# A transformer block on images: the first layer norm without its mean, the projection put into the attention's weights

## Chip, cores and metric

The kernel runs on one core of a Trainium2 chip, in fp32. The metric is the device time in microseconds of one execution; the kernel before takes 4315.69 us (median of 3 runs, 4314.87 to 4317.05). The profiled execution has a span of 4311.6 us. The core's engines are named as in the profile: PE (TensorE, matmuls and transposes), DVE (VectorE), ACT (ScalarE), POOL (GpSimd), SP (SyncE, which here only issues DMAs).

## The reference

x has 16 images of 128 channels by 96 x 96 pixels. Per image:

```python
xn1 = layernorm(x over channels) * ln1_w + ln1_b
q, k, v = xn1 @ wq.T, xn1 @ wk.T, xn1 @ wv.T      # 8 heads of 16 channels
q, k = l2norm over all 9216 pixels
attn = softmax(q @ k.T * scale)                   # 16 x 16 per head: channels, not pixels
x = x + (attn @ v) @ wp.T
xn2 = layernorm(x over channels) * ln2_w + ln2_b
h1 = w_in @ xn2                                   # 1x1, 128 -> 512 channels
h2 = depthwise 3x3 of h1
x = x + w_out @ gelu(h2)                          # 1x1, 512 -> 128 channels
```

The attention mixes channels, so an image needs of q and k only the Gram matrix of its normed pixels: G = sum over pixels of z z^T, and the sum s of z, with z the normed pixel. Everything up to the mixing matrix then is arithmetic on 128 x 128 matrices, once per image.

## The kernel before, in words

*Layout.* x lies with channels in the partitions. A layer norm is over channels, so pixels are turned into the partitions, normed there, and turned back. Both norms are made by one function, `norm(i, second, ...)`; norm a (`second` false) is LN1, norm b is LN2. Norm a of an image runs while the feed-forward network of the image before is computed, norm b a few bands ahead of its own image's network.

*One batch of a norm* is 4 tiles of 128 pixels; an image has 18 batches, and all 16 images 288 per norm. Its steps, with the name of the kind and the line of the profile:
- `forth`, PE L552: four transposes into a PSUM tile pT (two buffers).
- `stats`, DVE L559: two instructions that each give count, mean and variance sums of two tiles.
- `variance` and `power`, POOL L566 and L570: ve = var + eps, rstd = ve ** -0.5, four numbers per partition.
- `shift`, DVE L574: nb = -mean * rstd, four numbers per partition.
- `scaled`, ACT L591: zT = Identity(pT * rstd + nb), one activation per tile with two per-partition operands, scale and bias. In the first image's norm a, and in the first five batches of its norm b, DVE makes half of the tiles (L583, subtract mean, multiply by rstd).
- norm a only: `gram`, PE L601: G and s accumulate in one PSUM bank from zT with a column of ones.
- `back` and `place`, PE L631 and ACT L637 (norm a, plain copy) or L635 (norm b, with bias b2): zT turned back, 384 pixels at a time, and written as z into the padded buffers xn.

*Attention* (once per image, L697 to L796) goes from G and s over several small products on PE, copies on DVE, a power on POOL and one Exp on ACT to the mixing matrix mwT = w1 * (wv^T y) and to the vector d = (wv^T y)^T b1. Its weights are prepared once, by `weights`: wqkT is the transposed wq and wk with w1 multiplied in, cqk are the biases that b1 gives.
*Mixing* (L510): PE multiplies mwT with z, and d and x are added by ACT (L519) and a DMA that accumulates, or by DVE (L516).

*The feed-forward network* works on bands of 12 rows, 128 in all, in four chunks of 128 hidden channels. PE makes the hidden channels (L821), ACT copies them to SBUF (L826, `kept`). A 3x3 depthwise convolution is nine taps: ACT makes a few as products (L837, one into h3, two or three into buffers pr that a DMA adds), DVE makes the rest (L841, one instruction of 1152 elements per tap). ACT applies gelu (L849). In 66 of the 128 bands the fourth chunk is made by PE instead (L892, nine accumulated products, gelu at L898). PE multiplies with w_out (L915) and DVE adds x (L922).

*The order.* Nothing of this is ordered by a queue at run time. `Plan` collects every piece of work with its engine, a cost in ns, the tokens that it reads and writes and a place; the place is a job number plus an offset per kind from the table `AT`. `order()` simulates the engines: whenever one is free it takes the ready piece with the smallest place, where a piece is ready when its inputs are there (with a `SLACK` of 300 ns between engines) and its buffer is free. The program is written in that order, and each engine then runs its own instructions in this order. So the offsets in `AT`, the costs given to `dve(...)`, `act(...)`, `pe(...)`, and the buffers (two for pT, four PSUM banks h, three zT, five pr) decide what stands behind what.

Of the kernel before, what the change touches and what calls it, by code (L numbers as in the profile page):

```python
# [9 lines left out]
F32 = mybir.dt.float32  # L10
# [21 lines left out]
AT = dict(  # L32
    weights=11.05, zeros=-2.3, load_a=-22.85, forth_a=-15, stats_a=-11, variance_a=-7.95, power_a=3.5,
    shift_a=-15.95, scaled_a=-2.85, gram=-4.15, back_a=-20.9, place_a=-21.85, attention=-18.15, mix=-8.5,
    residual=-15.95, mixed=-8.45, add_x=12.05, forth_b=-12.4, stats_b=-8.15, variance_b=-11.85,
    power_b=-15.9, shift_b=-27.4, scaled_b=2.2, back_b=-22.2, place_b=-0.25, halo=6.25, hidden=0.55,
    kept=-7.05, product=-12.5, products=4.05, add_last=-15.5, tap=1.25, add_first=23.45, gelu=-16.4,
    conv=-0.5, conv_gelu=-14.15, out=3.65, add=-2.4, store=-0.9,
)
# [166 lines left out]
def tile_restormer_block(  # L206
# [21 lines left out]


    nc = tc.nc  # L230
    B, C, H, W = x.shape
# [48 lines left out]
    nc.scalar.dma_start(out=dw, in_=w_dw.rearrange("(n p) o kh kw -> p n (o kh kw)", p=P))  # L280

    none = const.tile([P, 1], F32, name="none")
    wqkT = const.tile([P, 2 * P], F32, name="wqkT")
# [113 lines left out]
    def weights(p):  # L397
# [4 lines left out]
        def loads():  # L402
            a, b = (h3p.tile([P, BR * W], F32, tag="h3", name=f"weights_{k}") for k in range(2))
            v["win"] = a[:, :HID].rearrange("p (n c) -> p n c", c=P)
            v["wout"], v["wp"] = a[:, HID : 2 * HID], a[:, 2 * HID : 2 * HID + P]
            v["wqk"], v["wqkT"] = b[:, : 2 * P], b[:, 2 * P : 4 * P]
            v["wt"] = b[:, 4 * P : 8 * P].rearrange("p (t c) -> p t c", c=P)
            nc.scalar.dma_start(out=v["wqk"][:, :P], in_=wq)
            nc.scalar.dma_start(out=v["wqk"][:, P:], in_=wk)
            nc.scalar.dma_start(out=v["wp"], in_=wp)  # L410
            nc.scalar.dma_start(out=v["win"], in_=w_in.rearrange("(n p) c kh kw -> p n (c kh kw)", p=P))
            nc.scalar.dma_start(out=v["wout"], in_=w_out.rearrange("c j kh kw -> c (j kh kw)"))
# [15 lines left out]
        def keep_qkp(pt):  # L428
            nc.vector.tensor_copy(v["wqkT"], pt[:, : 2 * P])
            nc.vector.tensor_scalar(wqkT, pt[:, : 2 * P], w1, None, ALU.mult)  # L430
            nc.vector.tensor_copy(wpT, pt[:, 2 * P : 3 * P])

        def biases():
# [9 lines left out]
        def shifts():  # L443
# [9 lines left out]
        transposed(  # L453
            lambda: [v["wqk"][:, :P], v["wqk"][:, P:], v["wp"]], keep_qkp, ["qk"]
        )
        pe(440, at("weights", p), biases, [("w", "qk"), mine[1]], [("h", ("weights", "biases"))])
        dve(400, at("weights", p), lambda: nc.vector.tensor_copy(cqk, v["pc"]), [("h", ("weights", "biases"))], [("w", "qk")])
        transposed(
            lambda: [v["win"][:, n, :] for n in range(NCH)],
# [34 lines left out]
    def norm(i, second, place_of):  # L494
# [41 lines left out]
        def pixels(s, m):  # L536
# [43 lines left out]
            def also_scaled(q):  # L580
                for k in range(by_dve):
                    t = (q - qs[0]) * QT + k
                    nc.vector.tensor_scalar(  # L583
                        zT(q)[:, k, :P], d["pT", q][:, k, :], d["mv"][:, t, 1:2], d["rstd"][:, t : t + 1],
# [3 lines left out]
            def scaled(q):  # L588
                for k in range(by_dve, QT):
                    t = (q - qs[0]) * QT + k  # L590
                    nc.scalar.activation(  # L591
                        zT(q)[:, k, :P], d["pT", q][:, k, :], AF.Identity,
# [20 lines left out]
            op("POOL", T_POWER, at("power" + ab, s), power, [], [bt], T_POWER + 33 + SLACK)  # L613
            dve(80, at("shift" + ab, s), shift, [], [bt])
            for h, (q, tr) in enumerate(zip(qs, trs)):
                zt, sh = ("zT", (name, q)), s + STEP["scaled"] * h
                if by_dve:
                    dve(by_dve * 240, at("scaled" + ab, sh), lambda q=q: also_scaled(q), [tr, bt], [(*zt, 0)])
                act((QT - by_dve) * 343, at("scaled" + ab, sh), lambda q=q: scaled(q), [tr, bt], [(*zt, 1)])
                if not second:  # L620
# [48 lines left out]
    def attention(s, i):  # L669


        places_of = dict(srow="ma", kq="ma", em="ma", y="ma", gs="mb", e="mb", a="mb", mT="mb")
        columns = dict(ps_s=128, ps_u=256, ps_r=0, ps_n=128, ps_kq=256, ps_qk=384, ps_y=0, ps_m=128, ps_d=256)
# [105 lines left out]

        @step("PE", 220)  # L780
        def _():
            nc.tensor.matmul(ps([P, P], "ps_m"), lhsT=wv_sb, rhs=v["y"], start=True, stop=True)

        @step("DVE", 400)
        def _():
            nc.vector.tensor_scalar(sb([P, P], "mwT", keep), v["ps_m"], w1, None, ALU.mult)
            nc.vector.tensor_copy(sb([P, P], "mT"), v["ps_m"])

        @step("PE", 220)
        def _():  # L790
            nc.tensor.matmul(ps([P, 1], "ps_d"), lhsT=v["mT"], rhs=b1, start=True, stop=True)

        @step("DVE", 80)
        def _():
            nc.vector.tensor_copy(sb([P, 1], "d", keep), v["ps_d"])
# [204 lines left out]
```

## Time and profile before

| | PE | DVE | ACT | POOL |
|---|---|---|---|---|
| busy, us | 4216.3 | 4190.5 | 4149.9 | 2427.5 |
| share of the span | 98% | 97% | 96% | 56% |
| instructions | 17446 | 5086 | 7256 | 2309 |
| share of the chain that ended last | 46% | 13% | 32% | 2% |

Busy time is the time in which at least one instruction of the engine is under way. Instructions of one engine overlap at their ends, so an engine's busy time is more than the sum of the steps from one start to the next. The chain that ended last is followed back from the last instruction: at each step to what released it, or to the instruction before it on its engine. PE's granted clock is 0.996 of full speed on the mean. The DMA engines are at 0.90 of their time in the long middle of the run, mostly with the products that are added by DMA.

The groups of norm a, with the busy time of each, from the profile's groups:

| kind | engine, line | count | busy us | mean ns of one |
|---|---|---|---|---|
| forth | PE L552 | 1080 | 164.8 | 276 |
| stats | DVE L559 | 540 | 228.0 | 423 |
| variance | POOL L566 | 288 | 286.2 | 994 |
| power | POOL L570 | 288 | 497.0 | 1726 |
| shift | DVE L574 | 288 | 44.8 | 156 |
| scaled | ACT L591 | 1080 | 434.2 | 569 |
| gram | PE L601 | 2304 | 306.8 | 276 |
| place | ACT L637 | 384 | 227.1 | 591 |

(72 tiles of the first image are in groups of their own for forth and stats, and 36 more activations for scaled. A product in fp32 is two passes of PE, so gram has two per tile.)

### The profile page before, as it was taken

The numbers are of one execution on the slowest core, as the hardware profiler recorded it, in microseconds if no ns is written. First come the engines' busy times: TensorE is split into PE (matmuls) and PEld (weight loads), VectorE is DVE, ScalarE is ACT, GpSimd is POOL, SyncE is SP. The second block draws the span as 40 slices with busy tenths as digits, with TensorE's granted clock in tenths as the row PEclk, the third lists the DMA queues.
The fourth block names the chain that finished last, engine by engine and source line by source line (L and its number), as shares of the span: only waits on it lengthen the run. The fifth ranks groups of instructions, "written<-read, shape, count | busy, mean of one in ns | idle before, by whom it ended". The sixth has DMA issues, their size and how long they took to land.

```text
span 4311.6 us, 52468 instructions
## 1 busy us (share of the span) xinstructions
PE 4216.3 (98%) x17446; PEld 2686.8 (62%) x17446; DVE 4190.5 (97%) x5086; ACT 4149.9 (96%) x7256; POOL 2427.5 (56%) x2309
## 2 busy tenths in 40 slices
PE   8999999999999999999999999999999999999999
PEld 6666666666666666666666666666666666666555
DVE  6999999999999999999999999999999999999999
ACT  5999999999999999999999999999999999999996
POOL 3555556555565655656556555655655556556342
PEclk9999999999999999999999999999999999999999
DMA  2889898998989999889898998989989898888887
GB/s 85 174 182 197 184 188 183 187 193 183 190 179 191 192 185 190 188 187 194 183 189 179 194 192 182 191 175 194 194 180 194 176 200 184 185 185 175 178 182 165
DMA packets 194719, 789.89 MB, mean 183 GB/s; under 512 B 22544, under 2 KB 23952, under 8 KB 194448
## 3 DMA queue, kind: packets, MB, share of 16 engines
q0 software_dynamic: 154944, 634.72, 78.0%
q1 hardware_dynamic: 37152, 151.01, 9.6%
q8 instruction: 138, 2.26, 0.2%
q10 hardware_dynamic: 2352, 0.81, 0.1%
q14 instruction: 133, 1.09, 0.1%
HBM read 148.26 MB, written 75.50 MB: 52 GB/s over the span
## 4 chain that ended last, share of the span: by engine, by line
PE 46%; ACT 32%; DVE 13%; DMA 4%; issue 3%; POOL 2%; ACTq 0%; POOLq 0%; DVEq 0%
PE h L915 13%; PE h L892 12%; DVE h L841 10%; PE h L821 9%; ACT pr L837 8%; ACT zT L591 6%; ACT h L826 4%; ACT h L837 4%; ACT h L849 4%; DMA h<-pr 4%; PE g L601 3%; PE h L510 2%; ACT x L519 2%; PE pB_a L631 1%; ACT xn L635 1%
## 5 line engine op out<-in xcount | busy, mean ns | idle before, releaser
L841 DVE SCALAR_TENSOR_TENSOR h<-h,dw,h 128x1152 f32<-128x1152 f32 x2614 | 3593.6, 1407 | 2.8 <-ACT h L837 1.2
L837 ACT ACTIVATE pr<-h,dw 128x1152 f32<-128x1152 f32 x954 | 1291.4, 1369 | 3.8 <-DMA pr<-pr 3.7
L892 PE MATMUL h<-xn,comp 128*128 128x384 f32 x3564 | 1284.7, 487 | 3.5 <-DVE x L922 2.5
L915 PE MATMUL h<-h,woutT 128*128 128x384 f32 x3072 | 1143.9, 493 | 25.3 <-ACT h L826 17.0
L821 PE MATMUL h<-xn,winT 128*128 128x384 f32 (+1 forms) x2676 | 1047.3, 502 | 13.4 <-ACT h L826 7.5
L892 PEld LDWEIGHTS h<-xn,comp 128*128 128x128 f32 x3564 | 653.3, 189 | 430.7 <-issue 27.1
L915 PEld LDWEIGHTS h<-h,woutT 128*128 128x128 f32 x3072 | 562.0, 192 | 385.9 <-issue 28.5
L845 POOL DMA_DIRECT2D pr<-pr x509 | 480.5, 944 | 521.0 <-ACT pr L837 434.1
L826 ACT COPY h<-h 128x384 f32<-128x384 f32 (+1 forms) x1338 | 712.2, 588 | 39.0 <-PE h L821 26.2
L845 POOL DMA_DIRECT2D h<-pr x445 | 427.7, 963 | 562.7 <-DVE h L841 139.9
L821 PEld LDWEIGHTS h<-xn,winT 128*128 128x128 f32 x2676 | 485.9, 190 | 333.8 <-issue 28.4
L837 ACT ACTIVATE h<-h,dw 128x1152 f32<-128x1152 f32 x446 | 602.1, 1350 | 1.7
L849 ACT ACTIVATE h<-h 128x1152 f32<-128x1152 f32 x448 | 561.8, 1254 | 32.1 <-DMA h<-pr 28.4
L570 POOL TENSOR_TENSOR rstd_b<-ve_b,mhalf 128x4 f32<-128x4 f32 x288 | 513.8, 1784 | 11.8
L570 POOL TENSOR_TENSOR rstd_a<-ve_a,mhalf 128x4 f32<-128x4 f32 x288 | 497.0, 1726 | 13.5 <-POOL ve_a L566 0.2
L566 POOL TENSOR_SCALAR ve_b<-st_b 128x4 f32<-128x4 f32 x288 | 298.2, 1035 | 326.9 <-DVE st_b L559 321.3
L591 ACT ACTIVATE zT<-pT_b,nb_b,rstd_b 128x128 f32<-128x128 f32 x1132 | 454.2, 566 | 5.1 <-DVE nb_b L574 4.9
L566 POOL TENSOR_SCALAR ve_a<-st_a 128x4 f32<-128x4 f32 x288 | 286.2, 994 | 291.5 <-DVE st_a L559 287.5
L591 ACT ACTIVATE zT<-pT_a,nb_a,rstd_a 128x128 f32<-128x128 f32 x1080 | 434.2, 569 | 9.9 <-DVE nb_a L574 9.5
L601 PE MATMUL g<-zT 128*128 128x129 f32 x2304 | 306.8, 276 | 0.0
L510 PE MATMUL h<-xn,mwT 128*128 128x384 f32 x768 | 295.5, 490 | 4.1 <-ACT h L826 2.9
L601 PEld LDWEIGHTS g<-zT 128*128 128x128 f32 x2304 | 286.1, 192 | 15.3 <-issue 2.1
(145 smaller groups left out, 3761.0 us busy)
## 6 DMA issues: line engine op xcount, KB each, us to landing
pr<-pr POOLq DMA_DIRECT2D x509, 576.0 KB, 6.2
h<-pr POOLq DMA_DIRECT2D x445, 576.0 KB, 6.9
x<-in_x_dram SPq DMA_DIRECT2D x128, 576.0 KB, 6.0
out_dram<-x SPq DMA_DIRECT2D x127, 576.0 KB, 5.3
x<-in_x_dram POOLq DMA_DIRECT2D x122, 576.0 KB, 7.2
out_dram<-x SPq DMA_DIRECT2D x3, 192.0 KB, 1.9
weights<-in_L_conv_w_in_dram ACTq DMA_DIRECT2D x1, 256.0 KB, 10.8
weights<-in_L_conv_w_out_dram ACTq DMA_DIRECT2D x1, 256.0 KB, 11.7
```

Source lines behind the costliest of these rows:

```text
L566: nc.gpsimd.tensor_scalar(ve, d["mv"][:, :, 2], 1.0 / C, EPS, ALU.mult, ALU.add)
L570: nc.gpsimd.tensor_tensor(rstd, d["ve"], mhalf, ALU.pow)
L591: nc.scalar.activation(zT(q)[:, k, :P], d["pT", q][:, k, :], AF.Identity, bias=d["nb"][:, t : t + 1], scale=d["rstd"][:, t : t + 1],)
L601: nc.tensor.matmul(grams[i][:, : P + 1], lhsT=zt[:, :P], rhs=zt, start=(q == 0 and k == 0), stop=(q == NU * TPU // QT - 1 and k == QT - 1),)
L821: nc.tensor.matmul(rows(ph), lhsT=winT[:, n, :], rhs=window(xn, r0 + r, e - r, 1), start=True, stop=True)
L826: nc.scalar.copy(window(h1_, r, e - r, 1), rows(d.pop(("ph", r))))
L837: nc.scalar.activation(to, shifted(t), AF.Copy, scale=dw[:, n, t : t + 1])
L841: nc.vector.scalar_tensor_tensor(h3, shifted(t), dw[:, n, t : t + 1], h3, ALU.mult, ALU.add)
L845: nc.gpsimd.dma_start(out=to, in_=d["pr", t], accum_op=ALU.add)
L849: nc.scalar.activation(h3, h3, AF.Gelu)
L892: nc.tensor.matmul(d["pc"], lhsT=comp[:, t, :], rhs=window(xn, r0 + dy, UR, dx), start=(t == 0), stop=(t == 8),)
L915: nc.tensor.matmul(rows(d["po"]), lhsT=woutT[:, n, :], rhs=h3s[g, n][:, s * UR : (s + 1) * UR, :], start=(k == 0), stop=(k == NCH - 1),)
```

## The change

The mean of LN1 need not be taken from every pixel. With M = I - 1/128 (the matrix that takes the mean off a vector of channels), (x - mean) * rstd = M (x * rstd). Since all uses of z in the attention and in the mixing are products with weights, M can be multiplied into the weights once. So zT in norm a is x * rstd alone; wqkT, wv and, with them, mwT carry M and w1; and d comes from wv b1, made once, instead of from a product with b1 per image. The variance is still that about the mean. Norm b stays as it was.

Parts:
- norm a has no `shift` on DVE; `scaled` is a Copy with a scale and no bias, its planned cost falls from 343 to 250 ns per tile. DVE's share in the first image multiplies only.
- `weights` has a fourth transpose (wv), three small products and copies to make the centred weights.
- `attention` has one step less on PE and one less on DVE: the product for d goes with that for mwT, and both are copied by one step.
- `AT` has new offsets for nearly all kinds.

```diff
 AT = dict(
-    weights=11.05, zeros=-2.3, load_a=-22.85, forth_a=-15, stats_a=-11, variance_a=-7.95, power_a=3.5,
-    shift_a=-15.95, scaled_a=-2.85, gram=-4.15, back_a=-20.9, place_a=-21.85, attention=-18.15, mix=-8.5,
-    residual=-15.95, mixed=-8.45, add_x=12.05, forth_b=-12.4, stats_b=-8.15, variance_b=-11.85,
-    power_b=-15.9, shift_b=-27.4, scaled_b=2.2, back_b=-22.2, place_b=-0.25, halo=6.25, hidden=0.55,
-    kept=-7.05, product=-12.5, products=4.05, add_last=-15.5, tap=1.25, add_first=23.45, gelu=-16.4,
-    conv=-0.5, conv_gelu=-14.15, out=3.65, add=-2.4, store=-0.9,
+    weights=12.1, zeros=-4.25, load_a=-26.7, forth_a=-14, stats_a=-11.05, variance_a=-12.7, power_a=1.65,
+    scaled_a=0.7, gram=-13.35, back_a=-23.05, place_a=-22.45, attention=-22.4, mix=-10.1,
+    residual=-10.05, mixed=-5.05, add_x=7.55, forth_b=-12.8, stats_b=-4.35, variance_b=-11.8,
+    power_b=-15.45, shift_b=-38.75, scaled_b=5.45, back_b=-24.35, place_b=-0.45, halo=10.5, hidden=0.35,
+    kept=-6.8, product=-16.15, products=7.15, add_last=-10.8, tap=1.6, add_first=9.35, gelu=-15,
+    conv=-0.7, conv_gelu=-16.6, out=3.65, add=-3.95, store=-2.6,
 )
...
+            nc.vector.tensor_copy(v["wvT"], pt[:, 3 * P :])
+            nc.vector.tensor_scalar(v["centre"], ident, -1.0 / C, None, ALU.add)
+            nc.vector.tensor_scalar(v["w1centre"], v["centre"], w1, None, ALU.mult)
+
+        def centred():
+            pc = v["pc2"] = bank(("weights", "centred"))
+            nc.tensor.matmul(pc[:, : 2 * P], lhsT=v["centre"], rhs=wqkT, start=True, stop=True)
+            nc.tensor.matmul(pc[:, 2 * P : 3 * P], lhsT=v["wvT"], rhs=v["w1centre"], start=True, stop=True)
+            nc.tensor.matmul(pc[:, 3 * P : 3 * P + 1], lhsT=v["wvT"], rhs=b1, start=True, stop=True)
+
+        def keep_centred():
+            nc.vector.tensor_copy(wqkT, v["pc2"][:, : 2 * P])
+            nc.vector.tensor_copy(wv_sb, v["pc2"][:, 2 * P : 3 * P])
+            nc.vector.tensor_copy(wvb, v["pc2"][:, 3 * P : 3 * P + 1])
...
             def also_scaled(q):
...
+                    if not second:
+                        nc.vector.tensor_scalar(
+                            zT(q)[:, k, :P], d["pT", q][:, k, :], d["rstd"][:, t : t + 1], None, ALU.mult
+                        )
+                        continue
...
             def scaled(q):
...
+                    if not second:
+                        nc.scalar.activation(
+                            zT(q)[:, k, :P], d["pT", q][:, k, :], AF.Copy, scale=d["rstd"][:, t : t + 1]
+                        )
+                        continue
...
-            dve(80, at("shift" + ab, s), shift, [], [bt])
+            if second:
+                dve(80, at("shift" + ab, s), shift, [], [bt])
...
-                act((QT - by_dve) * 343, at("scaled" + ab, sh), lambda q=q: scaled(q), [tr, bt], [(*zt, 1)])
+                act((QT - by_dve) * (343 if second else 250), at("scaled" + ab, sh), lambda q=q: scaled(q), [tr, bt], [(*zt, 1)])
...
-        @step("PE", 220)
+        @step("PE", 300)
         def _():
             nc.tensor.matmul(ps([P, P], "ps_m"), lhsT=wv_sb, rhs=v["y"], start=True, stop=True)
-
-        @step("DVE", 400)
-        def _():
-            nc.vector.tensor_scalar(sb([P, P], "mwT", keep), v["ps_m"], w1, None, ALU.mult)
-            nc.vector.tensor_copy(sb([P, P], "mT"), v["ps_m"])
-
-        @step("PE", 220)
-        def _():
-            nc.tensor.matmul(ps([P, 1], "ps_d"), lhsT=v["mT"], rhs=b1, start=True, stop=True)
-
-        @step("DVE", 80)
-        def _():
+            nc.tensor.matmul(ps([P, 1], "ps_d"), lhsT=v["y"], rhs=wvb, start=True, stop=True)
+
+        @step("DVE", 290)
+        def _():
+            nc.vector.tensor_copy(sb([P, P], "mwT", keep), v["ps_m"])
             nc.vector.tensor_copy(sb([P, 1], "d", keep), v["ps_d"])
             mats[i] = v["mwT"], v["d"]
```

More of the change, by code (lines that the diff above doesn't have):

```diff
@@ L280, in tile_restormer_block @@
     nc.scalar.dma_start(out=dw, in_=w_dw.rearrange("(n p) o kh kw -> p n (o kh kw)", p=P))
+    wvb = const.tile([P, 1], F32, name="wvb")
     none = const.tile([P, 1], F32, name="none")
@@ L407, in loads @@
             v["wt"] = b[:, 4 * P : 8 * P].rearrange("p (t c) -> p t c", c=P)
+            v["centre"], v["w1centre"], v["wvT"] = b[:, 8 * P : 9 * P], b[:, :P], b[:, P : 2 * P]
             nc.scalar.dma_start(out=v["wqk"][:, :P], in_=wq)
@@ L453, in weights @@
         transposed(
-            lambda: [v["wqk"][:, :P], v["wqk"][:, P:], v["wp"]], keep_qkp, ["qk"]
+            lambda: [v["wqk"][:, :P], v["wqk"][:, P:], v["wp"], wv_sb], keep_qkp, ["qk"]
         )
@@ L457, in weights @@
         dve(400, at("weights", p), lambda: nc.vector.tensor_copy(cqk, v["pc"]), [("h", ("weights", "biases"))], [("w", "qk")])
+        pc = ("h", ("weights", "centred"))
+        pe(1000, at("weights", p), centred, [("w", "qk"), mine[1]], [pc])
+        dve(800, at("weights", p), keep_centred, [pc], [("w", "qk")])
         transposed(
@@ L669, in attention @@
     def attention(s, i):
-        places_of = dict(srow="ma", kq="ma", em="ma", y="ma", gs="mb", e="mb", a="mb", mT="mb")
+        places_of = dict(srow="ma", kq="ma", em="ma", y="ma", gs="mb", e="mb", a="mb")
         columns = dict(ps_s=128, ps_u=256, ps_r=0, ps_n=128, ps_kq=256, ps_qk=384, ps_y=0, ps_m=128, ps_d=256)
```

## The prediction

> **What bounds the kernel now.** I read the page's busy shares first. Three engines are close to full, so the share alone names none of them:
>
> ```profile
> PE 4216.3 (98%) x17446; PEld 2686.8 (62%) x17446; DVE 4190.5 (97%) x5086; ACT 4149.9 (96%) x7256; POOL 2427.5 (56%) x2309
> ```
>
> Second, the table by stage, with the span cut into a start, a long middle and an end (columns: stretch, length, then busy us and count of PE, PEld, DVE, ACT, POOL, then clock, DMA share, GB/s):
>
> ```profile
> 0.00:108.00 108.00, 91.34 (x571) 74.38 (x572) 71.56 (x207) 61.31 (x138) 43.09 (x103) 0.95 0.27 86
> 108.00:4200.00 4092.00, 4017.76 (x16536) 2549.70 (x16535) 4014.59 (x4790) 4010.91 (x7009) 2359.05 (x2180) 1.00 0.90 186
> 4200.00:4312.00 112.00, 107.22 (x342) 62.70 (x340) 104.33 (x92) 77.64 (x111) 25.39 (x28) 1.00 0.78 164
> ```
>
> The middle holds 95% of the time, and there PE, DVE and ACT are each idle for only 74 to 81 us of 4092. Busy time counts the tail of an instruction that the next one overlaps, so I took from the chain of waits how long one instruction really holds its engine when another stands behind it:
>
> ```profile
> 2000.18 1.40 ACT zT L591 x4
> 2003.19 0.37 ACT xn L637
> 2022.09 3.87 PE h L892 x12
> 2042.61 0.07 DVE nb_a L574
> 2043.15 1.33 DVE h L841
> 2044.48 0.34 DVE st_b L559
> 2098.15 0.48 ACT xn L635
> ```
>
> With these steps and the counts of the page the engines' work is:
> - DVE: 2614 taps x 1.326 + 1152 statistics x 0.341 + 384 adds x 0.467 + 576 shifts x 0.073 + about 85 for sixteen attentions and the early tiles = about 4165 us.
> - PE: 9640 passes of 384 columns x 0.3225 + 440 of 480 x 0.403 + 6912 of 128 or 129 x 0.109 + about 75 = about 4115 us.
> - ACT: 1400 products x 1.147 + 2258 scalings x 0.342 + the copies, gelus and placings at 0.24 to 1.05 each = about 4055 us.
>
> So DVE carries most. Over the whole span it has 4311.6 - 4165 = 147 us without work; 36 of them lie in the start (108 - 71.6) and 8 in the end. In the middle its waits are few, and two rows are most of them (engine, tile and line <- what it waited for: us, times, longest):
>
> ```profile
> DVE nb_a L574 <- POOL rstd_a L570: 25.7, 25, 2.0
> DVE nb_b L574 <- POOL rstd_b L570: 25.4, 26, 2.0
> DVE x L922 <- PE h L915: 5.4, 16, 0.6
> ```
>
> DVE runs out of inputs from ACT or PE for under 20 us in 4092. It is the engine that sets the pace of the middle, and the tiny instruction nb, four numbers per partition, causes most of the waiting it does. One such place in DVE's own order of time:
>
> ```profile
> 2057.56 0.16 DVE L574 SCALAR_TENSOR_TENSOR nb_a<-st_a,rstd_a 128x4 f32<-128x4 f32 x1
> 2057.64 2.74 DVE L841 SCALAR_TENSOR_TENSOR h<-h,dw,h 128x1152 f32<-128x1152 f32 x2
> 2061.28 0.16 DVE L574 SCALAR_TENSOR_TENSOR nb_a<-st_a,rstd_a 128x4 f32<-128x4 f32 x1 [0.90 <-POOL rstd_a L570]
> 2061.35 4.07 DVE L841 SCALAR_TENSOR_TENSOR h<-h,dw,h 128x1152 f32<-128x1152 f32 x3
> ```
>
> Three taps stand behind an nb that waits 0.90 us for POOL's power. Last, the groups that the change touches (busy us, mean ns | idle before, releaser):
>
> ```profile
> L591 ACT ACTIVATE zT<-pT_a,nb_a,rstd_a 128x128 f32<-128x128 f32 x1080 | 434.2, 569 | 9.9 <-DVE nb_a L574 9.5
> L574 DVE SCALAR_TENSOR_TENSOR nb_a<-st_a,rstd_a 128x4 f32<-128x4 f32 x288 | 44.8, 156 | 27.9 <-POOL rstd_a L570 27.9
> ```
>
> **What the Trainium skill says.** "ScalarE: Activation LUTs", section What ACT_TABLE_LOAD costs: every per-partition pointer operand of an activation adds about 93 ns. The trace agrees: placing 384 columns takes 0.48 us with a bias column (L635) and 0.37 us as a plain copy (L637), 0.11 us apart. "PSUM — Partial Sum Buffer", section Engine vs sequencer instructions: the queues of ScalarE, VectorE and GpSimdE are strict first-in-first-out. The trace agrees, as the taps behind the waiting nb show. "Perfetto Trace Analysis", section Identifying the Most-Contended Engine: occupancy is a fair measure for Vector and Scalar, but not for matmuls. That is why PE's 98% above doesn't make it the bound for me: it has 17446 passes, which at the steps above come to 4115 us, 95% of the span.
>
> **The change part by part.**
> 1. *DVE loses 288 nb_a* (18 batches x 16 images): 288 x 0.073 = 21 us of work on the engine that sets the pace.
> 2. *DVE loses their wait*, 27.9 us over the span. What stood behind, taps and statistics, can start at once where its inputs are there, and the waits view says that they nearly always are. Bounds: 0 (the same time comes back as other waits) to 27.9. I take 24: PE and ACT have to follow a DVE that is 1% faster, and will sometimes be late.
> 3. *The wait moves to ACT.* zT now needs rstd from POOL directly, and the scaling stands at the head of ACT's queue, with kept copies (L826), placings and products behind it; PE and then DVE wait for those. What POOL's lateness costs ACT I bound by what DVE had to wait, 28 us, and from below by 0, as before ACT only waited 9.9 us for nb_a and had one hop more in between. I take 20.
> 4. *ACT's scaling gets cheaper*: 1080 + 36 activations lose the bias pointer. At 0.093 (skill) to 0.11 us (L635 against L637) that is 104 to 123 us; I take 104. A scaling falls from 0.35 to about 0.25 us. ACT's work drops to about 3950 us, which more than pays for the 20 us of 3. It lies beside DVE's work and I count nothing of it directly: DVE waited for ACT for only some 5 us. It makes steps 1 and 2 possible, since ACT at 4055 us would have had little room to follow.
> 5. *The early DVE scaling* (36 tiles, first image) keeps one instruction per tile with one operand less: no change that the 0.32 us per tile from PSUM would show.
> 6. *Attention*, 16 times: mwT becomes a plain copy (0.26 to 0.20 us) and the copy mT (0.20) goes: 16 x 0.26 = 4 us of DVE work. PE keeps both products, and one hop PE-DVE-PE goes. In the middle the attention is hidden among taps and matmuls, so I count only the 4 us.
> 7. *Weights*, once: PE gets one transpose (0.11) and three products (2 x 0.215 + 2 x 0.11 + 2 x 0.03 = 0.7 us); DVE six small copies, about 1.2 us. In 40 to 60 us DVE is idle for 6.6 us of 20, so its part is hidden; PE carries the chain there with few gaps, so I count 0.8 us. The hop saved in the first attention gives about as much back: 0 in sum.
> 8. *The order* (new places for nearly all kinds). No row prices it. Each kind moves by some job-lengths among others that are ready at once; I take 0, with ±15 us for the range, a guess of some 30% of the 51 us that both nb made DVE wait in the middle.
>
> Sum: -21 - 24 - 4 = -49 us, 4315.7 - 49 = 4267 us.
>
> **The rivals.**
> - *PE takes over.* For: PE's work of 4115 us leaves 196 us, and from 4150 to 4294 us the chain of waits is PE in nearly every piece. Against: in the middle it is at 96% by steps. Then only PE's own waits shrink. In the middle those named for ACT's zT are 6.1 + 5.3 + 4.0 + 2.8 = 18 us: 4298 us. DMA (share 0.90 of 16 engines in the middle) would end in the same place.
> - *More than the sum.* ACT's 104 us of slack also lets kept copies and placings come earlier and clears the remaining small waits. The floor is DVE's new work, 4140, plus 44 in start and end, plus the 25 us for nb_b that stay: 4209. Half way from 4267 to that is 4238 us. For: ACT holds 32% of the chain of waits. Against: DVE hardly waited for ACT.
> - *Slower.* The moved wait weighs more, because the new order asks for rstd too early: if ACT waited 1 us (the mean of the 25 waits that DVE had) at each of 288 scalings, its load would be 3950 + 288 = 4238, with the 47 us idle in its start and 34 at its end 4319 us, and the late copies would add something: about 4330 us. Against: the planner still allows for the power's time and a slack before zT.
>
> **How the numbers follow.** Chances: forecast 0.58, PE takes over 0.20, more than the sum 0.13, slower 0.09. The likeliest gives 4267. A range of 4238 to 4304 takes in the first three with the ±15 of the order and the bound of 0 for step 2 (4291), and leaves out the slower case and the ends of the others. Faster by over 0.2% means under 4307: the first and third and nearly all of the second, 0.88; within 0.2%, 0.04; slower, 0.08.
>
> **What would show it right or wrong.** Right: nb_a and its wait are gone from DVE, its work in the middle is over 97% of the time, and its waits there are under 55 us; zT of norm a takes about 1.0 us for four, ACT's busy time is some 100 us less, and ACT waits for rstd_a for 10 to 30 us in all. Wrong: DVE waits as long as before, but for other things (then step 2 fails); zT hardly gets shorter (step 4); ACT waits far over 30 us for rstd_a (step 3); the chain goes through PE for far over 46% (first rival).

## The result, and the profile after

The change takes 4293.25 us (median of 4 runs, 4288.81 to 4298.51), and the kernel before, beside it, 4315.82 us: a ratio of 0.9948 [0.9931, 0.9965], 22.6 us or 0.5% faster. The forecast was 4267 us, 49 us faster. The direction held and the time lies in the range, but less than half of the expected gain came. The profiled run has a span of 4287.6 us.

Page of the kernel after, busy us, share and instructions of each engine:

```profile
PE 4200.7 (98%) x17453; PEld 2681.0 (63%) x17453; DVE 4165.3 (97%) x4788; ACT 4066.4 (95%) x7256; POOL 2477.1 (58%) x2309
```

ACT lost 83 us of busy time, DVE 25 us and 298 instructions; PE has 7 passes more and 16 us less busy time. The table by stage of the kernel after, cut at the same places (columns as before; this span ends at 4287.6 us, within the third stretch):

```profile
0.00:108.00 108.00, 91.88 (x555) 73.45 (x556) 68.28 (x184) 53.85 (x132) 43.87 (x101) 0.94 0.26 82
108.00:4200.00 4092.00, 4026.00 (x16645) 2559.85 (x16644) 4017.92 (x4540) 3961.97 (x7058) 2418.57 (x2192) 1.00 0.89 188
4200.00:4312.00 112.00, 82.83 (x255) 47.73 (x254) 79.13 (x66) 50.53 (x69) 14.67 (x17) 0.99 0.52 114
```

DVE fills the middle as it did (4018 against 4015 us of 4092); ACT now has 130 us of idle time there instead of 81. The start is no shorter: the first tap begins at 95.1 us (96.0 before). The groups that the change touches, kernel after (busy us, mean ns | idle before, releaser):

```profile
L594 DVE SCALAR_TENSOR_TENSOR nb_b<-st_b,rstd_b 128x4 f32<-128x4 f32 x288 | 45.1, 157 | 40.7 <-POOL rstd_b L590 40.7
...
L617 ACT ACTIVATE zT<-pT_a,rstd_a 128x128 f32<-128x128 f32 x1080 | 327.5, 448 | 16.4 <-POOL rstd_a L590 16.0
```

nb_a is gone and its 27.9 us of waiting with it; zT of norm a has lost 107 us of busy time. But nb_b, which the change doesn't touch, waits for 40.7 us instead of 25.6. What DVE waits for in the middle, kernel after (us, times, longest):

```profile
DVE nb_b L594 <- POOL rstd_b L590: 40.7, 39, 2.0
DVE x L946 <- PE h L939: 8.8, 16, 1.8
DVE st_b L579 <- PE pT_b L572: 5.0, 12, 0.8
DVE st_a L579 <- PE pT_a L572: 5.0, 13, 0.6
DVE h L865 <- ACT h L861: 3.1, 5, 1.4
```

The five lines are 62.6 us; the five longest of before came to 63.0. Other waits have taken the place of the removed one: nb_b (+15), statistics that find no transposed pixels, taps that find no product of ACT. I add up the idle time ahead of all DVE instructions over the span: 118.2 us before and 119.3 after. The rest of the span is called DVE's work here: 4311.6 - 118.2 = 4193.4 before, 4287.6 - 119.3 = 4168.3 after. (A wait so short that the overlap of two instructions hides it counts as work in this account; the prediction's 4165 us for before, a sum of steps, leaves such waits out.) So the profiled spans differ by 24 us, and DVE's own work by 25: DVE's idle time is no smaller for the wait that was removed. This is bookkeeping. It doesn't say which part of the change earned the 24 us; the experiments with single parts below do.

The chain of waits after, around one nb_b and one zT of norm a (start us, us, what):

```profile
2947.74 0.43 DVE st_b L579
...
2950.29 1.33 DVE h L865
2951.62 0.03 POOLq L869
2951.65 0.01 POOL ve_b L586
2951.66 0.46 issue
2952.12 0.02 POOLq L869
2952.14 0.88 POOL h L869
2953.02 0.90 POOL pr L869
2953.92 3.22 POOL rstd_b L590
2957.14 0.02 issue
2957.17 0.17 DVE nb_b L594
...
2971.40 2.43 POOL rstd_a L590
2973.83 0.02 issue
2973.85 1.14 ACT zT L617 x4
```

A tap still takes 1.33 us and statistics 0.34; four zT take 1.14 us where they took 1.40. The piece of chain from 2951.6 to 2957.2 us is POOL: the small ve_b, two DMA issues that stand between it and the power, and the power, 3.22 us here and 1.0 us at its shortest. Then nb_b is released, and DVE's next residual addition and taps with it.

### The profile page after: what moved, and what is told of

It reads as the page before. It is cut to its first block, busy times and chain, and to the rows that moved or that the text cites. A ratio compares the mean times of both kernels' runs of the same rounds, so it can differ in the third digit from the quotient of the medians.

```text
span 4287.6 us, 52224 instructions
## 1 busy us (share of the span) xinstructions
PE 4200.7 (98%) x17453; PEld 2681.0 (63%) x17453; DVE 4165.3 (97%) x4788; ACT 4066.4 (95%) x7256; POOL 2477.1 (58%) x2309
## 5 line engine op out<-in xcount | busy, mean ns | idle before, releaser
L916 PE MATMUL h<-xn,comp 128*128 128x384 f32 x3564 | 1262.9, 486 | 14.0 <-DVE x L946 6.5
L861 ACT ACTIVATE pr<-h,dw 128x1152 f32<-128x1152 f32 x954 | 1256.8, 1335 | 6.0 <-DMA pr<-pr 5.7
L939 PE MATMUL h<-h,woutT 128*128 128x384 f32 x3072 | 1122.9, 488 | 19.5 <-ACT h L850 10.3
L845 PE MATMUL h<-xn,winT 128*128 128x384 f32 (+1 forms) x2676 | 1067.3, 502 | 10.7 <-ACT x L539 4.2
L850 ACT COPY h<-h 128x384 f32<-128x384 f32 (+1 forms) x1338 | 684.5, 554 | 58.2 <-PE h L845 47.9
L873 ACT ACTIVATE h<-h 128x1152 f32<-128x1152 f32 x448 | 545.2, 1217 | 46.7 <-DMA h<-pr 43.1
L861 ACT ACTIVATE h<-h,dw 128x1152 f32<-128x1152 f32 x446 | 585.9, 1314 | 3.1
L586 POOL TENSOR_SCALAR ve_b<-st_b 128x4 f32<-128x4 f32 x288 | 337.7, 1173 | 230.6 <-DVE st_b L579 227.8
L586 POOL TENSOR_SCALAR ve_a<-st_a 128x4 f32<-128x4 f32 x288 | 306.1, 1063 | 273.6 <-DVE st_a L579 270.2
L617 ACT ACTIVATE zT<-pT_a,rstd_a 128x128 f32<-128x128 f32 x1080 | 327.5, 448 | 16.4 <-POOL rstd_a L590 16.0
```

Of the source, the lines that this page charges most:

```text
L586: nc.gpsimd.tensor_scalar(ve, d["mv"][:, :, 2], 1.0 / C, EPS, ALU.mult, ALU.add)
L845: nc.tensor.matmul(rows(ph), lhsT=winT[:, n, :], rhs=window(xn, r0 + r, e - r, 1), start=True, stop=True)
L850: nc.scalar.copy(window(h1_, r, e - r, 1), rows(d.pop(("ph", r))))
L861: nc.scalar.activation(to, shifted(t), AF.Copy, scale=dw[:, n, t : t + 1])
L873: nc.scalar.activation(h3, h3, AF.Gelu)
L916: nc.tensor.matmul(d["pc"], lhsT=comp[:, t, :], rhs=window(xn, r0 + dy, UR, dx), start=(t == 0), stop=(t == 8),)
```

## The experiments

The kernel before took between 4307 and 4337 us on the chips used, so I compare ratios to the runs of before on the same chip, and turn them into us with 4316. "DVE's idle time" and "DVE's work" are those defined above, in the profiled run of each kernel.

**Is the new order to blame?** The change's code with the offsets of before, and the code of before with the new offsets. The diff shows the first lines of the table; all other offsets go back too.

```diff
 AT = dict(
-    weights=12.1, zeros=-4.25, load_a=-26.7, forth_a=-14, stats_a=-11.05, variance_a=-12.7, power_a=1.65,
+    weights=11.05, zeros=-2.3, load_a=-22.85, forth_a=-15, stats_a=-11, variance_a=-7.95, power_a=3.5,
...
```

> The changed kernel with the offsets of before (AT of before, everything else of the change kept). Theory 1, the new order ate the gain: about 4267 us, the forecast, with DVE waiting 25 us for nb_b. Theory 2, DVE's idle time of some 118 us stays whatever waits are removed, and only its work counts: 4290 us as for the changed kernel, +-10 for an order that nobody fitted to the new costs.

> The kernel before with the offsets of the change (shift_a, which the change has no more, keeps -15.95). Theory 1, the new order costs what the removed wait should have given: 4316 + 25 = about 4340 us. Theory 2, the order is worth little by itself: 4316 us +-10.

Measured: 0.994 [0.9925, 0.9955] for the new code with the old offsets, 1.0046 [1.0031, 1.0061] for the old code with the new ones. The second is 20 us slower than before: on the old code the new offsets cost time. On the new code they bring nothing that can be told (0.9948 with them, 0.994 without). With the old offsets nb_b's wait is back at 21.3 us in the middle, but the additions then wait 14.1 us for PE and the statistics of norm b 9.8 us; DVE's idle time is 114 us all the same. Between these two runs of the new code the offsets decide which wait it is, hardly how much.

**What is the removed wait worth alone?** In the kernel before, nb_a is made from the mean only, so that it no longer waits for the power; then both nb. The diff is that of the second; in the first only norm a's nb is so changed. In both the shift is no longer the layer norm's; they only price the wait.

```diff
-                nc.vector.scalar_tensor_tensor(nb, d["mv"][:, :, 1], -1.0, d["rstd"], ALU.mult, ALU.mult)
+                nc.vector.scalar_tensor_tensor(nb, d["mv"][:, :, 1], -1.0, d["mv"][:, :, 1], ALU.mult, ALU.mult)
```

> The kernel before, same order, same work: nb_a on DVE is made from the mean alone (-mean x mean, so norm a's shift is not LN1's) and no longer waits for POOL's power; ACT's scaling then waits for the power itself. Prediction's step 2, the wait is DVE time lost: 27.9 us of waits go, 24 of them gained, 4292 us. Theory 2, other waits take the place: 4312 to 4318 us, DVE's idle time still about 118 us.

> As the run before, for nb_a and nb_b (both norms' shifts are made from the mean alone and are not the layer norms'). Step 2: 53.5 us of DVE's waits go, at 24/28 of them gained 4270 us. Theory 2: 4308 to 4318 us, with DVE waiting for ACT's and PE's results instead.

Measured: 0.9977 [0.9967, 0.9987] without nb_a's wait, 0.9958 [0.9941, 0.9974] without both. That is 10 us of 27.9, and 18 us of 53.5: a third each time, with some 4 and 7 us of doubt. In the first, DVE's idle time falls by 10 us too (118.2 to 108.2), and nb_b waits 5 us more. The other two thirds of the wait were not gained: other waits came in their place.

**The change's two reliefs, one by one.** All in the order of before: nb_a gone but ACT keeps a pointer (to zeros); the pointer gone but nb_a still made; both. None of the three takes the mean off, so they only price the parts.

```diff
             def shift():
+                if not second:
+                    return
...
+                    if not second:
+                        nc.scalar.activation(
+                            zT(q)[:, k, :P], d["pT", q][:, k, :], AF.Copy, scale=d["rstd"][:, t : t + 1]
+                        )
+                        continue
...
-                        bias=d["nb"][:, t : t + 1], scale=d["rstd"][:, t : t + 1],
+                        bias=d["nb"][:, t : t + 1] if second else zero, scale=d["rstd"][:, t : t + 1],
```

The first of the three has the first and the last of these edits, the second has the middle one, the third the first and the middle one.

> The kernel before, its own order to the letter, without the instruction nb_a on DVE; ACT keeps its bias pointer, to a column of zeros, so the mean stays in LN1's output (the weights are not centred). DVE loses 21 us of work and 28 us of waits, ACT nothing. By the prediction's steps 1 to 3: -45 us, 4271. By the runs so far (the wait worth a third, the work up to a half): -15 to -21, about 4298.

> The kernel before, its own order to the letter, nb_a still made on DVE, but ACT's scaling of norm a is a Copy with scale alone and doesn't read it (the mean stays in LN1's output). ACT loses 1116 x 0.098 = 109 us of work, and DVE keeps nb_a with its wait for the power. By the prediction's step 4, ACT's relief counts nothing by itself: within 4 us of before. If ACT is worth as much as putting the pointer back cost in the changed kernel (0.4 us per us): -43, about 4273.

> Both of the last two at once, in the order of before (the mean stays in LN1's output, nothing is made up for it in the weights). By the prediction: 4267 to 4271. If the two reliefs add: about -20 - 43 = 4253. If one stands in for the other (both only end the same hold-ups): no more than the larger of the two, and near 4290 as with the change.

Measured: 0.9974 [0.9963, 0.9985], 0.9955 [0.9939, 0.9972] and 0.99 [0.9886, 0.9915]: 11, 19 and 43 us faster. What follows:
- Taking DVE's work and wait away, 49 us by the groups of before, is worth 11 us as long as ACT keeps its load. DVE's idle time even rises from 118 to 125 us.
- Relieving ACT by some 104 us, with DVE's work untouched, is worth 19 us, and DVE's idle time falls from 118 to 96 us. DVE scarcely has waits for ACT by name. Of the 22 us, 12 are at the two nb (19.8 and 19.3 us in the middle, 25.4 and 25.7 before), which wait for POOL by name; by what way ACT's relief gets there isn't shown.
- Both together are worth more than the sum of 30 us, by 13 us; the intervals, put together as independent ones, leave about 11 us of doubt on that.

The page of the kernel with both gone:

```profile
span 4269.7 us, 52307 instructions
...
PE 4195.5 (98%) x17446; PEld 2687.0 (63%) x17446; DVE 4168.7 (98%) x4798; ACT 4065.6 (95%) x7256; POOL 2424.8 (57%) x2309
```

ACT and DVE have the busy times of the change within 4 us, and the span is 18 us shorter; DVE's idle time is 98 us. In this order steps 1 and 2 of the prediction came out nearly as said: 22 us of work and 20 us of waiting.

**The relief of ACT, put back.** The change, with a bias pointer to zeros.

```diff
-                            zT(q)[:, k, :P], d["pT", q][:, k, :], AF.Copy, scale=d["rstd"][:, t : t + 1]
+                            zT(q)[:, k, :P], d["pT", q][:, k, :], AF.Identity,
+                            bias=zero, scale=d["rstd"][:, t : t + 1]
```

> The changed kernel, same order, but norm a's scaling on ACT is Identity with a bias column of zeros again: 1116 x 0.098 = 109 us more ACT work, nothing else. If ACT's relief only makes room, as the prediction's step 4 has it: 5 to 15 us slower than the change. If ACT's relief is what made the change faster: 25 us slower, back at 4315. If ACT doesn't matter at all: within 3 us.

Measured: 1.0055 [1.0039, 1.0071], 46 us slower than the change and 24 us slower than before. So ACT's load is on the path for nearly half of its size, though no wait of DVE for ACT is large. What DVE waited for in the middle of this run:

```profile
DVE nb_b L596 <- POOL rstd_b L592: 49.7, 51, 2.0
DVE x L949 <- PE h L942: 19.8, 41, 3.6
DVE st_a L581 <- PE pT_a L574: 13.4, 24, 1.5
DVE st_b L581 <- PE pT_b L574: 12.4, 24, 1.3
```

ACT's load comes back to DVE under the names of POOL and PE: each of these rows is 7 to 11 us longer than in the change's table, and DVE's idle time is 168 us.

**The other two engines.** PE with one tap of nine less in the fourth chunk's convolution (128 us of passes); and one four-element DVE instruction more per batch of norm a, behind its statistics.

```diff
+            if t == 4:
+                return
             dy, dx = divmod(t, 3)
```

```diff
+                if j == 1 and not second:
+                    means = d["st"].rearrange("p j (t v) -> p (j t) v", v=3)[:, :, 1]
+                    dead = small.tile([P, QB * QT], F32, tag="dead", name=f"dead_{name}_{m}")
+                    nc.vector.scalar_tensor_tensor(dead, means, -1.0, means, ALU.mult, ALU.mult)
```

> The changed kernel, same order, with PE's work cut: the middle tap (4) of the nine in PE's depthwise convolution is left out, so that part of the fourth chunk's convolution is missing in 66 of 128 bands. 198 products x 0.645 us = 128 us less for PE. Theory PE (DVE sets the pace, PE is so close behind that DVE's removed waits turn into waits for PE): DVE's waits for PE (about 40 us) and some of the slack go, 20 to 40 us faster than the change, 4250 to 4270. Theory 2 (DVE alone, its idle time stays for other reasons): within 6 us of the change. Theory 3 (PE is the bound): 100 us faster or more.

> The changed kernel, same order, with one more DVE instruction of 4 elements per batch of norm a, right after the statistics, waiting for nothing and read by nobody: 288 x 0.073 = 21 us of DVE work. If DVE sets the pace (prediction's step 1): 17 to 21 us slower than the change. If DVE and PE share the pace: about half, 8 to 14 us. If PE does: 0 to 4 us.

Measured: 0.9922 [0.9899, 0.9946], about 11 us faster than the change, with some 12 us of doubt, for 128 us of PE work; and 0.9973 [0.9964, 0.9983], about 11 us slower for 42 us more of DVE work between the profiled spans (4169.8 in the change's second run, below, to 4211.8). The 42 us are twice the 21 expected, because the instruction does wait: DVE starts it 0.03 us after the end of the statistics that it reads, where a tap starts some 0.08 us before their end. PE alone doesn't set the pace, or most of the 128 us would have come; the low end of the 20 to 40 us expected of a PE that makes DVE wait is just within the doubt. DVE isn't alone on the path either: its idle time fell from 126.5 to 92.6 us, so most of what was added went into time that it had waited. Something else happened in that run. The instruction ve_a on POOL, all of it (duration ns shortest/median/longest), first in the change, then with the added DVE instruction:

```profile
L586 POOL TENSOR_SCALAR ve_a<-st_a x288: 184/1274/5261, 9.3 to 3899.9; 128x4 f32<-128x4 f32 x144
```

```profile
L590 POOL TENSOR_SCALAR ve_a<-st_a x288: 187/197/3083, 9.6 to 3916.8; 128x4 f32<-128x4 f32 x144
```

The median falls from 1.27 to 0.20 us. One place in each engine's order of time, first POOL's, then DVE's, in the run with the added instruction (start us, us, engine, line, instruction):

```profile
2000.24 0.20 POOL L590 TENSOR_SCALAR ve_a<-st_a 128x4 f32<-128x4 f32 x1 [1.60 <-DVE st_a L579]
...
2006.43 1.28 POOL L590 TENSOR_SCALAR ve_b<-st_b 128x4 f32<-128x4 f32 x1
```

```profile
2000.18 0.16 DVE L585 SCALAR_TENSOR_TENSOR dead_a<-st_a 128x4 f32<-128x4 f32 x1
2000.27 4.07 DVE L869 SCALAR_TENSOR_TENSOR h<-h,dw,h 128x1152 f32<-128x1152 f32 x3
...
2006.25 1.40 DVE L869 SCALAR_TENSOR_TENSOR h<-h,dw,h 128x1152 f32<-128x1152 f32 x1
```

ve_a starts beside the short instruction, 0.03 us ahead of the first tap; ve_b, which has no such opening, ends within 0.1 us of the tap that runs beside it. "SBUF — State Buffer" of the Trainium skill, section Who interferes with whom, says that a DVE instruction with two SBUF inputs contends with a GpSimd instruction that reads SBUF, and that the order of issue decides who blocks. A tap reads two tensors h from SBUF, and the durations agree: 0.20 us where ve_a starts first, and about one tap (1.33 us) where it doesn't.

**The change once more, and with nb_b moved to POOL.**

```diff
-                nc.vector.scalar_tensor_tensor(nb, d["mv"][:, :, 1], -1.0, d["rstd"], ALU.mult, ALU.mult)
+                nc.gpsimd.tensor_tensor(nb, d["nm"], d["rstd"], ALU.mult)
```

In the kernel with nb_b on POOL, POOL makes -mean too (nm), in a small instruction of its own behind ve_b.

> The changed kernel as it is, on the same chip as the next three, so that they can be set against it: 0.993 to 0.997 of the kernel before, about 4290 us.

> A try at a better version: the changed kernel with norm b's shift made on POOL in two instructions, -mean ahead of the power and times rstd after it, planned at 210 and 420 ns there; DVE has no nb_b. DVE loses 21 us of work and 41 us of waits; POOL (58% busy) gets 576 instructions more, and ACT's scaling of norm b waits for POOL. By a third of the waits and half of the work: -24 us against the change, about 4270. If POOL's queue makes rstd and nb late: same or slower than the change, up to 4310.

Measured: 0.9947 [0.9931, 0.9963] for the change, within 1 us of its first result, again with 41.0 us of waiting at nb_b in the middle; its DVE idle time is 126.5 us. With both nb off DVE, the time is 0.9982 [0.9975, 0.999]: 15 us slower than the change. The largest single wait of DVE is gone and 288 instructions with it, but DVE's work falls by only 6 us (4169.8 to 4164.0), not by the 21 expected, and its idle time is 138 us: statistics now wait 31 us for transposes in the middle (10 to 14 us in the two runs of the change), taps 16 us for ACT's products. ACT waits 24 us for POOL's nb_b, and POOL is busy for 67% of the span instead of 58%. A wait is moved here as it was by the change, and this time it costs more at its new place.

**One order, the work of the change.** The two reliefs in the old order gave 43 us, the change 23. What the run with both reliefs lacks of the change are the centred weights, the shorter attention, the new offsets and the new planned costs. So: the whole change with the offsets and the planned costs of before, its attention and weights in the planned pieces of before.

```diff
             def shift():
+                if not second:
+                    return
...
-            if second:
-                dve(80, at("shift" + ab, s), shift, [], [bt])
+            dve(80, at("shift" + ab, s), shift, [], [bt])
...
-                act((QT - by_dve) * (343 if second else 250), at("scaled" + ab, sh), lambda q=q: scaled(q), [tr, bt], [(*zt, 1)])
+                act((QT - by_dve) * 343, at("scaled" + ab, sh), lambda q=q: scaled(q), [tr, bt], [(*zt, 1)])
```

ACT, POOL and SP then have the order of the run with both reliefs, and DVE too but for the attention and the weights.

> All work of the change (centred weights and the attention's shorter tail), but in the order of before: AT of before, the planner still reckons with 343 ns a scaling and with a shift of norm a, whose place stays empty; the attention keeps its two last steps on PE and DVE, and the centred weights are made inside the step that keeps cqk. If the re-made order cost the 20 us: 4266 to 4276 us, the fastest so far. If the weights or the attention cost them: 4285 to 4295.

Measured: 0.9938 [0.9922, 0.9954], runs between 4279 and 4306 us: 27 us faster, not 43. So with nearly the same order and slightly less work it is some 16 us slower than the run with both reliefs, and far less steady (that one lay between 4271.8 and 4273.5). In its profiled run (span 4303.6, the longest of its six), much of the loss stands behind POOL. POOL's, DVE's and ACT's order of time, one place:

```profile
2724.22 11.91 POOL L588 TENSOR_SCALAR ve_a<-st_a 128x4 f32<-128x4 f32 x1
2736.08 0.88 POOL L878 DMA_DIRECT2D h<-pr  x1
2736.67 1.36 POOL L592 TENSOR_TENSOR rstd_a<-ve_a,mhalf 128x4 f32<-128x4 f32 x1
```

```profile
2723.68 0.44 DVE L581 BATCH_NORM_STATS2 st_a<-pT_a 128x6 f32<-128x256 f32 x1
2724.02 12.05 DVE L874 SCALAR_TENSOR_TENSOR h<-h,dw,h 128x1152 f32<-128x1152 f32 x9
2740.41 0.43 DVE L581 BATCH_NORM_STATS2 st_b<-pT_b 128x6 f32<-128x256 f32 x1 [4.34 <-PE pT_b L574]
```

```profile
2738.07 1.14 ACT L621 ACTIVATE zT<-pT_a,rstd_a 128x128 f32<-128x128 f32 x4 [6.19 <-POOL rstd_a L592]
```

Nine taps run without a break; ve_a, four numbers per partition, is under way through all nine, 11.91 us. Its power comes late, ACT stands 6.19 us at zT, PE gets its next transposes late, and at last DVE itself stands 4.34 us at the statistics. Of POOL's small norm instructions (ve and rstd of both norms), 12 lasted over 3.5 us in this run, together 84.5 us; in the run with both reliefs 6, together 24.5 us; before 6 and 23.4; in the change 10 and 40.4. I add up what of DVE's idle time lies under these long ones or in the 12 us behind each: 32.9 of 133 us in this run, 6.6 of 98 in the run with both reliefs. So here some 26 of the 35 us more stand beside them. In the change it is 11.5 of 119 us, before 6.9 of 118: about 5 us of what the forecast missed.

**Planned costs and empty places, one at a time.** The work of the change is the same in three more orders: new offsets with the old planned cost of 343 ns and an empty place for norm a's shift; old offsets with 343 ns only; old offsets with the empty place only. The edits are the parts of the diff just shown.

> The changed kernel with its own offsets, but the planner reckons with 343 ns a scaling and holds an empty place for norm a's shift (shift_a=-15.95). If the old costs were a slack that the hardware needs: 4270 to 4278. If the fit of the offsets to the order matters, and any change of costs under them only shuffles it: 4285 to 4305.

> The changed kernel with the offsets of before and 343 ns a scaling in the plan, but no place for the shift. If the 343 ns carry the slack: 4268 to 4276. If not: 4285 to 4292, as with the offsets of before and all new costs.

> The changed kernel with the offsets of before and an empty place for norm a's shift in the plan (80 ns, and its hop of 420 ns between POOL and ACT), but 250 ns a scaling. If the hop carries the slack, so that ACT doesn't come to the scaling ahead of rstd: 4268 to 4276. If not: 4285 to 4292.

Measured: 0.9964 [0.9953, 0.9976], 0.9953 [0.9937, 0.9968], 0.9984 [0.9975, 0.9993]. Neither piece alone makes the old order better. Together with the change (0.9948), the old offsets (0.994) and the order of before (0.9938) these are six orders of the same work, and they lie between 0.9938 and 0.9984: 20 us. In the profiled runs of all six, the change's second run too, DVE's idle time is 114 to 136 us, where before had 118. Long instructions on POOL alone don't rank them: the old offsets with 343 ns had 11 in the profiled run, 58.3 us together, the old offsets alone 3 with 11.2 us, and the spans are 4284.0 and 4284.7 us, with 114 us of DVE's idle time in each.

**An opening for POOL, and its counterpart.** The change in the order of before, with the dead DVE instruction behind norm a's statistics; and the change with a dead instruction ahead of the statistics, where it lengthens DVE's work by 18 us (4187.7 against 4169.8) and opens nothing for ve_a.

```diff
+                if j == 0 and not second:
+                    dead = small.tile([P, QB * QT], F32, tag="dead", name=f"dead_{name}_{m}")
+                    nc.vector.scalar_tensor_tensor(dead, mhalf, -1.0, mhalf, ALU.mult, ALU.mult)
```

> The change in the order of before, with one more DVE instruction of 4 elements right after each of norm a's batches of statistics, read by nobody (it waits some 30 ns for them[...]; about 0.1 us a batch, 31 us in all). If POOL shut out by DVE's taps is what made that kernel slow and unsteady: norm a's ve falls to about 0.2 us, none of its POOL instructions lasts over 3.5 us, and the time is 4280 +-6 in spite of the work, with runs closer together. If not: 10 to 25 us slower than without, about 4305.

> The changed kernel, same order, with one more DVE instruction of 4 elements per batch of norm a ahead of the statistics (its inputs are constants, so it waits for nothing, 0.073 us a batch, 21 us in all; read by nobody). It opens nothing for POOL. If the opening is what softened the cost of the instruction behind the statistics (31 us of work for 10 us of time): this one costs nearly all of its 21 us, 4310 to 4316. If only a third of DVE's work counts anyway: 7 us, about 4300.

Measured: 0.9922 [0.9907, 0.9936] with the opening, runs between 4296.9 and 4301.0 where before took 4332.5 us. DVE has 41 us more of work than in the same order without it (4211.1 against 4170.4), and the kernel is no slower, rather some 7 us faster by the ratios, whose intervals overlap. ve_a in this run:

```profile
L592 POOL TENSOR_SCALAR ve_a<-st_a x288: 186/197/2409, 9.4 to 3899.8; 128x4 f32<-128x4 f32 x144
```

No small instruction of norm a lasts over 3.5 us any more, the statistics hardly wait, and DVE's idle time is 88 us instead of 133. This is the lowest ratio here of a kernel that computes the reference, though its interval still touches that of the change (0.9931 to 0.9965) at one end.

The counterpart settles little. 0.9953 [0.9935, 0.997] is 2 us above the change, with some 10 us of doubt on either side; an addition of 18 us on an engine that alone sets the pace would have shown. ve_a kept its 1.27 us, nb_b waited for 52.3 us, and DVE's idle time in the profiled run (the longest of four) was 133 us, not the 93 of the instruction behind the statistics. So the opening is what shortens ve_a. That it shortens DVE's waits too is likely but not shown, as the two instructions also differ in length, 18 and 42 us of work; and since 18 us without an opening cost as little, the small price of the first dead instruction can't be put down to the opening.

## Why the prediction was right in direction and less than half in size

- **Steps 1 and 6, less work on DVE:** the size held. 21 + 4 us were forecast, and DVE's work fell by 25. That each us of this work is a us of time didn't: nb_a gone with its work and its wait brought 11 us, and 42 us of added work cost 11.
- **Step 2, "DVE loses their wait":** this is the step that failed. 24 of 27.9 us were counted, its lower bound of 0 came true: DVE's idle time is 118 us before and 119 after, 126.5 in the change's second run, and no less than 114 in any of the six orders of the new work. Its ground was that what stands behind nb nearly always has its inputs, and that the waits view says so. That view tells who was late last, not who would have been late next. With nb_a's wait taken away alone, 10 of 28 us came; the sign that I named for this failure, waits in the middle as long as before for other things, is what the profile shows (62.6 us in five rows, against the limit of 55). That the time is within 2 us of the 4291 that the prediction gives for a step 2 of 0 is in part luck: DVE's work is worth less by itself than step 1 counts, and ACT's relief more than the 0 of step 4.
- **Step 3, the wait on ACT:** held. zT waits 16 us for rstd_a, of 10 to 30 forecast.
- **Step 4, the pointer:** the size held, 0.342 to 0.250 us a step by the trace, so 103 us of ACT's work. "I count nothing of it directly" didn't: alone it is worth 19 us, and putting it back costs 46. In the change itself more than half of the relief became waiting: ACT's idle time, taken like DVE's, rose from 157 to 216 us. The premise behind steps 2 and 4, one engine that sets the pace because it has the most work, is wrong here. DVE, PE and ACT were within 3% of each other before and hand work on through two transposition buffers, four banks and three zT. Per us of its own work, ACT's load was worth 0.2 to 0.4 us, DVE's 0.1 to 0.5 (the last with the wait of nb_a) and PE's 0.1, each with some 5 to 12 us of doubt in the time. Only relieving two of them at once, in the old order, came near the sum that I had worked out.
- **Steps 5 and 7:** nothing speaks against them; the first tap comes 0.9 us earlier.
- **Step 8, the order at 0 ±15 us:** held. On the new code the new offsets differ by 3 us from the old ones, within the doubt, and six orders of the new work lie within 20 us. All are at least 16 us above the two reliefs in the order of before. The spread between orders is nearly as large as the gain of the change.
- **The rivals:** "PE takes over" named 4298 us, nearer than the forecast, but for a reason that the runs don't bear out: 128 us less on PE bring about 11 us. Its sign, the chain's share of PE, can't be read: the chain after reaches back over little more than a third of the span. "More than the sum" was not seen. The run with both reliefs comes to 43 us, more than its two parts apart (30), but not more than the 45 of steps 1 and 2. "Slower" was not seen; ACT's waits for rstd_a stayed small.

Where did the expected 24 us go? Shown: into nb_b's wait and smaller ones; that the offsets choose which wait it is; that a POOL instruction behind unbroken taps is late by up to nine of them, and, at the place shown, that this comes back to DVE. Not shown: that this loop is the main reason why DVE waits as long as before. The run with the opening in the order of before speaks for it, the counterpart neither for nor against; the longest of these instructions stand beside only some 5 of the missing 24 us in the change, and what the many of about one tap cost isn't known. So why the other waits come in the place of the removed one stays open. Open as well: why the two reliefs alone run steadily at 43 us with nearly the same order in which the full change varies by 26 us.

## What to carry to other kernels

When three engines are within a few per cent of each other, don't count a removed wait as gained. Here a third of a wait came when it was removed alone, and none that could be seen in the whole change; so add up the idle time ahead of the instructions of each engine, before and after. Price the relief of every engine near the top, not only of the first. Where a small instruction on POOL feeds the others, look at its longest durations, not at its mean, and at what DVE runs beside it.

## What the hardware showed that I had not expected

A POOL instruction on four numbers per partition takes 0.20 us when DVE leaves it an opening, 1.27 us in the median when DVE runs taps back to back, and up to 11.91 us when nine of them follow each other without a break. One DVE instruction on four numbers, put behind the statistics that it reads, is enough of an opening; it adds some 0.15 us to DVE's work each time (42 us over 288). The spans of POOL are rough, but at the place shown ACT's and DVE's waits behind it are seen on those engines.
